# Four small edits in a fused attention and mixture-of-experts kernel: the order of two projections, one layout, one operand's memory, one copy's loop order

## The chip, the cores and the metric

The kernel runs on one core of one Trainium2 chip. The metric is the device time of one execution in microseconds (us). The core has TensorE (PE, matrix products; PEld are its weight loads), VectorE (DVE), ScalarE (ACT), GpSimd (POOL) and SyncE (SP, which issues the DMA transfers here). Each engine works through its own queue in order, and engines wait for each other by semaphores. SBUF is the on-chip memory of 128 partitions, PSUM the memory into which TensorE writes.

## The reference

The input x is (2, 128, 256, 256): two images of 128 channels. Everything is fp32.

```python
x = x + conv(ln_c(x), W_qkv, W_out, rel_height, rel_width)
t = to_tokens(x)                       # (2, 65536, 128)
t = t + ffn(ln_t(t), router_w, router_b, expert_w, expert_b)
x = from_tokens(t)
```

`conv` is windowed attention with 4 heads of 32 channels: queries from windows of 8 x 8 pixels, keys and values from overlapping windows of 12 x 12, relative position logits by height and width computed from the query, softmax, then an output projection. A fixed mask leaves only the pairs of query and key whose rows have the same parity and whose columns have the same parity, so the attention splits into four independent planes, one for each parity of row and column. `ffn` is a mixture of 8 experts (128 x 128 matrices): a softmax router, the two best experts for each token, their weights normalised to one. `ln_c` and `ln_t` subtract the mean over the 128 channels and divide by the standard deviation.

## The kernel before, in words

Channels lie on the 128 partitions. An image is cut into 32 strips of 8 pixel rows; a strip has four planes of 4 x 128 positions (`NQ` = 512). The main loop (line 809) makes one turn per plane, 256 in all, and 7 more at the end. In every turn n four things at different stages of the pipeline go on side by side:

- `scores` and `attend` of plane n: 16 matmuls (L474) put the relative position logits into PSUM with `keys` (a 0/1 matrix that spreads them) as the stationary and `au` as the moving operand; 64 matmuls (L491) add queries times keys; ScalarE takes the exponential (L499, `pT`); 8 matmuls (L512) give the row sums, 64 (L522) the weighted values. DVE then transposes and inverts the sums (L532 `sT`, L534, L537 `rT`) and scales (L542, `o`). The arrays are used in tiles: 4 heads on 32 partitions each, two halves of the windows beside each other.
- `project` of plane n + 1: the bias logits `pu` (L408), the value rows `pv` (`value_rows`, L350), the keys `pk` (L423) and the queries `pq` (L445), each a PSUM tile from the pool `ps_mm`, which has three buffers that are used in turn. Their readers: `uT`, a DVE transpose (L413), of `pu`; `vr`, a ScalarE copy (L358), of `pv`; `kcol`, ScalarE copies (L434, and L441 for the edges), of `pk`; `qs`, a ScalarE copy (L447), of `pq`. The same pool serves `plt` and `plg` (norms) and `po` (output projection), so a turn normally takes seven buffers in the order pu, pv, pk, pq, plt, plg, po.
- `shift` of plane n + 1: two copies (L392) move parts of `uT` into `auT`, and a DVE transpose (L397) makes `au`. The stream transpose turns blocks of 32 x 32.
- `norms`, `route`, `spread` and the expert products for pixel rows of the strips before. `norms` lets TensorE sum x and x squared over the channels (L580, `plt`), transposes the sums into another PSUM tile (L589, `plg`), and `rstd` (L222) makes the reciprocal standard deviation: L232 to L235 form the variance u plus eps, ScalarE takes a logarithm and an exponential (L236, L237), and L238, L239, L596 and L598 do one Newton step. `route` picks the experts (L613 to L645). `spread` (L648) transposes the gates (L651, `gT`) and sends them to DRAM (`gd`), from where SP fetches them broadcast to all partitions (`gb`, `sb`, `rb`). DVE makes six products `xe` of the tokens with a gate (L705), GpSimd two more, and TensorE multiplies them with the eight expert matrices (L714), summing in PSUM (`acc`); L720 adds the sum to x. Each fp32 matmul shows as two passes with a weight load each.

The order within a turn is written out by hand (`tc.manual_schedule`, L808): each engine's queue holds its instructions in the order in which the generator steps in lines 826 to 902 issue them. On TensorE it is: scores, pu, pv, pk, pq, experts 4, 6, 7, 5 of the strip under way, row sums and attention products, plt, experts 0, 1, 2 of the next, po, expert 3. On DVE: router, gT, uT, auT, au, xs, xe, sT to o, plg, `rstd`, the addition of po (L555). On GpSimd: product 5, the normalisation of a row for a coming strip (L276, `ln1`), in one turn of four a copy of halo rows (L250), product 7. A one-element write to the buffer (L686, L688) stands before each transfer of a gate, so that the transfer starts no earlier than that point of the ScalarE or DVE queue. SP's queue takes gd, the value rows to DRAM (L369, `vrows`), rb, sb, the value windows back (L381, `vwin`) and the gates.

`rstd` keeps u and r in SBUF tiles of 128 x 8. `au` has the layout (window m of 32, row a, column s), so that L474's moving operand is 8 pieces of 16 consecutive elements, while the transpose L397 writes with a step of 16 elements. `kcol` holds the keys of a pair of windows as 10 columns of 6 rows; L434 writes row by row, each element 6 behind the one before.

Of the kernel before, what the change touches and what calls it, by code (L numbers as in the profile page):

```python
# [11 lines left out]
F32 = mybir.dt.float32  # L12
AF = mybir.ActivationFunctionType
ALU = mybir.AluOpType
# [3 lines left out]
P = 128  # L18
# [25 lines left out]
KR, KC = 6, 10  # L44
# [7 lines left out]
def kernel(  # L52
# [16 lines left out]
    nc = tc.nc  # L69
    B, C, H, W = x.shape  # L70
    NS = H // R
    PR, PC = R // 2, W // 2
    NP = PC // 8
# [18 lines left out]
    def mm_tile(name):  # L92
        return ps_mm.tile([P, 512], F32, tag="mm", name=name)
# [121 lines left out]
    auT = []  # L215
# [3 lines left out]
        nc.gpsimd.memset(auT[i][:, :, :, KR + 6 : KR + 7], NEG)  # L219


    def rstd(p4, k0, k1, name):  # L222

        u, r = (
            small.tile([P, 2, NT], F32, tag=v, name=f"{v}_{name}")[:, k0:k1] for v in ("u", "r")
        )
        mean, sq = (
            p4[:, :, E + 2 * k0 + j : E + 2 * k1 : 2].rearrange("p t k -> p k t") for j in range(2)  # L230
        )
        nc.vector.tensor_copy(r, mean)  # L232
        nc.vector.tensor_tensor(u, r, mean, ALU.mult)
        nc.vector.scalar_tensor_tensor(u, u, -1.0, sq, ALU.mult, ALU.add)
        nc.vector.scalar_tensor_tensor(u, u, 0.0, epsc[:, k0:k1], ALU.max, ALU.add)  # L235
        nc.scalar.activation(r, u, AF.Ln, scale=4.0)  # L236
        nc.scalar.activation(r, r, AF.Exp, scale=-0.5)  # L237
        nc.vector.scalar_tensor_tensor(u, u, -4.0, r, ALU.mult, ALU.mult)  # L238
        nc.vector.tensor_tensor(u, u, r, ALU.mult)  # L239
        return r, u  # L240
# [145 lines left out]
    def shift(uT, n, state):  # L386

        for j in range(2):
            shifted = uT[:, :, :, NU * j + 3 : NU * j + 9]
            dims = [list(d) for d in shifted.ap]  # L390
            dims[1 + j][0] -= 1
            nc.vector.tensor_copy(  # L392
                auT[n % 2][:, :, :, 6 * j : 6 * j + 6],
                bass.AP(shifted.tensor, shifted.offset, dims),
            )
        au = work.tile([P, 2 * NP, PR, 4], F32, tag="au", name=f"au{n}")
        nc.vector.transpose(au.rearrange("p m a s -> p a s m"), auT[n % 2])  # L397
        state["au"] = au

    def project(n, state):  # L400

        i, pl = divmod(n, 4)
        xp = xn[i % 2][:, pl // 2, pl % 2]
        inner = xp[:, 1 : 1 + PR, 1 : PC + 1]
        kk = kcol[pl]

        pu = mm_tile(f"pu{n}")
        nc.tensor.matmul(pu, lhsT=wrel, rhs=inner, start=True, stop=True)  # L408
        state["sent"] = value_rows(n)
        yield  # L410

        uT = work.tile([P, PR, 4, 32], F32, tag="uT", name=f"uT{n}", bufs=1)
        nc.vector.transpose(uT, pu.rearrange("p (a m s) -> p a s m", a=PR, s=4))  # L413
        state["shift"] = lambda: shift(uT, n, state)
        yield

        rows = list(ln_rows(i))
        for part in (rows[-4:], rows[:-4]):
            if not part:
                continue  # L420
            pk = mm_tile(f"pk{n}_{part[0]}")
            m = len(part)
            nc.tensor.matmul(  # L423
                pk[:, : m * PC],
                lhsT=wk,
                rhs=xp[:, part[0] : part[0] + m, 1 : PC + 1],
                start=True,
                stop=True,
            )
            pk3 = pk[:, : m * PC].rearrange("p (r c) -> p r c", r=m)  # L430
            for k, at, m in runs(i, part):
                new = pk3[:, k - part[0] : k - part[0] + m]
                places = kk[:, :, 0:NK].rearrange("p t (c r) -> p t r c", r=KR)[:, :, at : at + m]
                nc.scalar.copy(places[:, 1 : NP - 1], windows(new[:, :, KC - 3 :], 0, NP - 2))  # L434

                ends = [places[:, 0, :, 1:], new[:, :, 0 : KC - 1]]
                for j, step in enumerate(((NP - 1) * SLOT - KR, PC - KC + 1)):
                    dims = [list(d) for d in ends[j].unsqueeze(1).ap]
                    dims[1] = [step, 2]
                    ends[j] = bass.AP(ends[j].tensor, ends[j].offset, dims)  # L440
                nc.scalar.copy(*ends)  # L441
        yield

        pq = mm_tile(f"pq{n}")
        nc.tensor.matmul(pq, lhsT=wq, rhs=inner, start=True, stop=True)  # L445
        qs = work.tile([P, 2 * NP, PR, 4], F32, tag="qs", name=f"qs{n}")
        nc.scalar.copy(  # L447
            qs.rearrange("p m a s -> p a m s"), pq.rearrange("p (a m s) -> p a m s", a=PR, s=4)
        )
        yield  # L450

        state.update(qs=qs, kk=kk, vv=vwin[n % 2])
        yield

    def windows(rows, n0, count):

        first = rows[:, :, 8 * n0 : 8 * n0 + KC].unsqueeze(1)
        dims = [list(d) for d in first.ap]
        dims[1] = [8, count]
        return bass.AP(first.tensor, first.offset, dims)  # L460

    def scores(n, state):


        qs, kk, au = state["qs"], state["kk"], state["au"]
        turn = place(n // 4, 0) // 2
        att = ps_att.tile([P, 4, 512], F32, tag="att", name=f"att{n}")
        sc = att[:, :, 0:HQ]
        for w in range(2):
            for half in range(2):  # L470
                rows = slice(half * SLOT, (half + 1) * SLOT)
                for h in range(HEADS):
                    hp = slice(h * DH, (h + 1) * DH)
                    nc.tensor.matmul(  # L474
                        sc[rows, h].rearrange("p (t w z) -> p t w z", w=2, z=16)[:, :, w],
                        lhsT=keys[hp, turn, w],
                        rhs=au[hp, half * NP + w : (half + 1) * NP : 2].rearrange(
                            "p t a s -> p t (a s)"
                        ),
                        start=(w == 0),  # L480
                        stop=False,
                    )
        for t in range(HP):
            if t == HP // 2:
                yield
            for half in range(2):
                rows = slice(half * SLOT, (half + 1) * SLOT)
                m0 = 2 * (half * HP + t)
                for h in range(HEADS):
                    hp = slice(h * DH, (h + 1) * DH)  # L490
                    nc.tensor.matmul(  # L491
                        sc[rows, h, 32 * t : 32 * t + 32],
                        lhsT=kk[hp, half * HP + t, :],
                        rhs=qs[hp, m0 : m0 + 2].rearrange("p m a s -> p (m a s)"),
                        start=False,
                        stop=(t == HP - 1),
                    )
        pT = work.tile([P, HEADS, HQ], F32, tag="pT", name=f"pT{n}", bufs=1)
        nc.scalar.activation(pT, att[:, :, 0:HQ], AF.Exp)  # L499
        state.update(att=att, pT=pT)  # L500
        yield
# [61 lines left out]
    def norms(f, c, nm):  # L563

        g = gboth[next(g_turn) % len(gboth)]
        srcs = []
        for j, src in ((0, f and rows_of(*f)), (2, c and ln1_src(*c))):  # L570
            if src is None:
                continue
            sq = work.tile([P, CH], F32, tag=f"sq{j}", name=f"sq{j}{nm}", bufs=1)
            nc.scalar.activation(sq, src, AF.Square)  # L574
            srcs += [(j, src), (j + 1, sq)]
        yield
        plt = mm_tile(f"plt{nm}")
        for j, src in srcs:
            for t in range(NT):
                nc.tensor.matmul(  # L580
                    plt[32 * t : 32 * t + 32, :P],
                    lhsT=rw[:, j],
                    rhs=src[:, t * P : (t + 1) * P],
                    start=(j == srcs[0][0]),
                    stop=(j == srcs[-1][0]),
                )
        yield
        plg = mm_tile(f"plg{nm}")
        nc.vector.transpose(plg[:, :P], plt[:, :P])  # L589
        p4 = plg[:, :P].rearrange("p (t e) -> p t e", e=32)  # L590
        k0, k1 = (0 if f else 1), (2 if c else 1)
        r, u = rstd(p4, k0, k1, nm)
        rs = None
        if f:
            rs = small.tile([P, NT], F32, tag="rs", name=f"rs{nm}")
            nc.vector.scalar_tensor_tensor(rs, u[:, 0], 3.0, r[:, 0], ALU.add, ALU.mult)  # L596
        if c:
            nc.vector.scalar_tensor_tensor(  # L598
                g[:, 1, :, 1], u[:, 1 - k0], 3.0, r[:, 1 - k0], ALU.add, ALU.mult
            )  # L600
        yield g, rs, p4
# [360 lines left out]
```

## Time and profile before

| what | value |
|---|---|
| median of three runs | 4380.1 us (4376.23 to 4390.58) |
| the profiled execution | 4380.58 us |
| its span in the profile | 4378.8 us |
| mean TensorE clock granted | 0.993 of full |
| TensorE busy | 4248.2 us, 97% |
| TensorE weight loads | 2454.2 us, 56% |
| VectorE busy | 3853.9 us, 88% |
| ScalarE busy | 1456.6 us, 33% |
| GpSimd busy | 1091.6 us, 25% |
| DMA | 1022.19 MB, 233 GB/s in the mean |

The span is that of one execution recorded by the hardware profiler; the time of that execution is 1.8 us longer, for what lies around it. A group of instructions is named by line, engine, operation and tiles (out<-in), followed by shapes, count, busy time, mean time of one, and the idle time of the engine ahead of it with what ended that idle time. In the timeline each row has start and length in us, and in square brackets how long the engine was idle before and what released it. Matmuls are pipelined, and their ends are modelled: a row of TensorE includes its way through the array, so starts tell more than ends.

### The profile page before, as it was taken

To read this page: it belongs to the slowest core of one execution; us is meant where nothing else is said; L and a number is where in the kernel's file an instruction comes from. 1 tells how busy PE (TensorE), PEld (TensorE's weight loads), DVE (VectorE), ACT (ScalarE), POOL (GpSimd) and SP (SyncE) were. 2 spreads that over 40 slices of the span, in tenths; PEclk is the share of its full clock that TensorE was granted. 3 is DMA by queue.
4 is the path that set the end of the run, shared out by engine and by line. 5 is a ranking of instruction groups with operands and counts; after the bars stand their busy time and mean duration, and the time that the engine had idled before them with its cause. 6 is when DMAs were issued, how large, how long until landed. Compare 5 with 4: busy or idle time off the path is not lost. (4 is left out here: it accounts for less than half of the span.)

```text
span 4378.8 us, 224652 instructions
## 1 busy us (share of the span) xinstructions
PE 4248.2 (97%) x94273; PEld 2454.2 (56%) x94273; DVE 3853.9 (88%) x11850; ACT 1456.6 (33%) x3774; POOL 1091.6 (25%) x1126
## 2 busy tenths in 40 slices
PE   7899999999999999999999999999999999999987
PEld 5455555555555555555555555555555555555553
DVE  5899889899888989989888889988998888999987
ACT  3333333333333333333333333333333333333321
POOL 1222222222222222222222222222222222222211
PEclk9999999999999999999999999999999999999999
DMA  4677778777777787777777787777777777777766
GB/s 114 210 240 240 244 235 243 241 237 244 233 244 240 244 244 233 243 232 244 238 241 234 240 244 236 243 236 243 238 240 243 236 242 232 244 238 239 243 191 191
DMA packets 824580, 1022.19 MB, mean 233 GB/s; under 512 B 137634, under 2 KB 409634, under 8 KB 823594
## 3 DMA queue, kind: packets, MB, share of 16 engines
q1 hardware_dynamic: 822864, 1007.52, 74.8%
q8 instruction: 769, 12.60, 1.2%
q14 instruction: 217, 1.78, 0.1%
q10 hardware_dynamic: 730, 0.29, 0.0%
HBM read 863.78 MB, written 143.75 MB: 230 GB/s over the span
## 5 line engine op out<-in xcount | busy, mean ns | idle before, releaser
L714 PE MATMUL acc<-xe,ew 128*128 128x512 f32 x4096 | 1916.8, 600 | 21.4 <-DVE gb L688 17.5
L714 PEld LDWEIGHTS acc<-xe,ew 128*128 128x128 f32 x4096 | 757.9, 190 | 941.4 <-issue 872.1
L705 DVE TENSOR_TENSOR xe<-xs,gb 128x512 f32<-128x512 f32 x1536 | 950.5, 686 | 11.8 <-DMA gb<-gd 1.4
L709 POOL COPY last<-xe 128x1 f32<-128x1 f32 x256 | 47.0, 184 | 3088.0 <-DVE gb L688 3081.0
L705 POOL TENSOR_TENSOR xe<-xs,gb 128x512 f32<-128x512 f32 x512 | 650.7, 1272 | 0.7 <-issue 0.5
L276 POOL TENSOR_TENSOR xn<-xt,rb 128x512 f32<-128x512 f32 x249 | 373.7, 1501 | 170.4 <-DMA rb<-gd 164.1
L491 PE MATMUL att<-qs,kcol 32*64 32x32 f32 x32768 | 398.2, 227 | 5.1 <-issue 5.1
L491 PEld LDWEIGHTS att<-qs,kcol 32*64 32x64 f32 x32768 | 395.9, 131 | 6.6 <-issue 6.2
L522 PEld LDWEIGHTS att<-pT,vwin 64*32 64x32 f32 x32768 | 350.2, 105 | 50.4 <-issue 11.8
L522 PE MATMUL att<-pT,vwin 64*32 64x32 f32 x32768 | 350.6, 200 | 8.0 <-issue 6.3
L350 PEld LDWEIGHTS pv<-wt,xn 128*128 128x128 f32 x2048 | 270.1, 192 | 126.5 <-issue 78.7
L434 ACT COPY kcol<-pk 128x560 f32<-128x560 f32 (+2 forms) x344 | 319.0, 927 | 52.8 <-PE pk L423 49.4
L499 ACT ACTIVATE pT<-att 128x1024 f32<-128x1024 f32 x256 | 261.8, 1023 | 208.0 <-PE att L491 207.2
L445 PE MATMUL pq<-xn,wt 128*128 128x512 f32 x512 | 274.7, 617 | 30.0 <-DVE uT L413 26.0
L574 ACT ACTIVATE sq<-xt 128x512 f32<-128x512 f32 x505 | 291.9, 629 | 0.0
L408 PE MATMUL pu<-xn,wrel 128*128 128x512 f32 x512 | 291.7, 651 | 0.0
L397 DVE STREAM_TRANSPOSE au<-auT 128x512 f32<-128x512 f32 x256 | 272.3, 1064 | 9.0
L550 PE MATMUL po<-o,wt 128*128 128x512 f32 x512 | 264.4, 598 | 8.4 <-DVE o L542 5.8
L350 PE MATMUL pv<-wt,xn 128*128 128x128 f32 x2048 | 271.2, 275 | 0.8 <-issue 0.8
L532 DVE STREAM_TRANSPOSE sT<-att 128x512 f32<-128x512 f32 x256 | 183.5, 717 | 98.7 <-PE att L522 84.7
L423 PE MATMUL pk<-xn,wt 128*128 128x512 f32 (+2 forms) x528 | 262.9, 582 | 1.3 <-DVE uT L413 1.3
L474 PEld LDWEIGHTS att<-au,keys 32*64 32x64 f32 x8192 | 117.9, 133 | 227.8 <-PE po L550 183.5
(2696 smaller groups left out, 4895.9 us busy)
## 6 DMA issues: line engine op xcount, KB each, us to landing
gb<-gd SPq DMA_DIRECT2D x2048, 256.0 KB, 5.8
vwin<-vrows SPq DMA_DIRECT2D x512, 240.0 KB, 5.4
xt<-in_x_dram SPq DMA_DIRECT2D x256, 256.0 KB, 6.6
sb<-gd SPq DMA_DIRECT2D x256, 256.0 KB, 4.1
out_dram<-xt SPq DMA_DIRECT2D x256, 256.0 KB, 6.2
rb<-gd SPq DMA_DIRECT2D x249, 256.0 KB, 3.4
vrows<-vr SPq DMA_DIRECT2D x168, 256.0 KB, 3.9
vrows<-vr SPq DMA_DIRECT2D x160, 128.0 KB, 3.5
```

The source lines that it names most:

```text
L276: eng.tensor_tensor(xn[i % 2][:, :, :, k, 1 : PC + 1], ln1_src(i, k).rearrange("p (y j x) -> p y x j", y=2, x=2), rb.rearrange("p (y j x) ...
L350: nc.tensor.matmul(pv[:, j * P : (j + 1) * P], lhsT=xp[:, k, 1 : PC + 1], rhs=wv, start=True, stop=True,)
L397: nc.vector.transpose(au.rearrange("p m a s -> p a s m"), auT[n % 2])
L408: nc.tensor.matmul(pu, lhsT=wrel, rhs=inner, start=True, stop=True)
L434: nc.scalar.copy(places[:, 1 : NP - 1], windows(new[:, :, KC - 3 :], 0, NP - 2))
L445: nc.tensor.matmul(pq, lhsT=wq, rhs=inner, start=True, stop=True)
L491: nc.tensor.matmul(sc[rows, h, 32 * t : 32 * t + 32], lhsT=kk[hp, half * HP + t, :], rhs=qs[hp, m0 : m0 + 2].rearrange("p m a s -> p (m a ...
L522: nc.tensor.matmul(av[hp, half, 32 * t : 32 * t + 32], lhsT=vv[rows, t, hp], rhs=pT[rows, h, 32 * t : 32 * t + 32], start=True, stop=True,)
L550: nc.tensor.matmul(po, lhsT=wo, rhs=state["o"].rearrange("p f z -> p (f z)"), start=True, stop=True)
L574: nc.scalar.activation(sq, src, AF.Square)
L705: eng.tensor_tensor(self.xe[e], self.xs, self.gb.pop(e), ALU.mult)
L714: nc.tensor.matmul(self.acc, lhsT=ew[:, e, :], rhs=self.xe.pop(e), start=(e == 0), stop=not self.xe)
```

## The change

1. In `project`, `value_rows(n)` is called ahead of the bias matmul `pu`: the order of the buffers becomes pv, pu, pk, pq.
2. `au` gets the layout (a, s, m), in which the transpose L397 writes consecutive elements. The moving operand of L474 becomes a strided view: m in steps of 2 elements, (a, s) in steps of 32 elements as the inner index.
3. `rstd` takes a piece of the PSUM tile `plg` behind its first 128 columns, and keeps u there. The product of the mean with itself goes to an SBUF tile m.
4. L434's copy goes through its elements with the row as the innermost index rather than the column.

The number and the sizes of instructions stay the same. Behind the first edit the lines of the changed file move by one to three.

```diff
-    def rstd(p4, k0, k1, name):
-        u, r = (
-            small.tile([P, 2, NT], F32, tag=v, name=f"{v}_{name}")[:, k0:k1] for v in ("u", "r")
+    def rstd(p4, room, k0, k1, name):
+        u = room.rearrange("p (k t) -> p k t", t=NT)[:, k0:k1]
+        r, m = (
+            small.tile([P, 2, NT], F32, tag=v, name=f"{v}_{name}")[:, k0:k1] for v in ("r", "m")
         )
...
         nc.vector.tensor_copy(r, mean)
-        nc.vector.tensor_tensor(u, r, mean, ALU.mult)
-        nc.vector.scalar_tensor_tensor(u, u, -1.0, sq, ALU.mult, ALU.add)
+        nc.vector.tensor_tensor(m, r, mean, ALU.mult)
+        nc.vector.scalar_tensor_tensor(u, m, -1.0, sq, ALU.mult, ALU.add)
...
-        au = work.tile([P, 2 * NP, PR, 4], F32, tag="au", name=f"au{n}")
-        nc.vector.transpose(au.rearrange("p m a s -> p a s m"), auT[n % 2])
+        au = work.tile([P, PR, 4, 2 * NP], F32, tag="au", name=f"au{n}")
+        nc.vector.transpose(au, auT[n % 2])
...
+        state["sent"] = value_rows(n)
         pu = mm_tile(f"pu{n}")
         nc.tensor.matmul(pu, lhsT=wrel, rhs=inner, start=True, stop=True)
-        state["sent"] = value_rows(n)
...
-                nc.scalar.copy(places[:, 1 : NP - 1], windows(new[:, :, KC - 3 :], 0, NP - 2))
+                nc.scalar.copy(
+                    places[:, 1 : NP - 1].rearrange("p t r c -> p t c r"),
+                    windows(new[:, :, KC - 3 :], 0, NP - 2).rearrange("p t r c -> p t c r"),
+                )
...
-                        rhs=au[hp, half * NP + w : (half + 1) * NP : 2].rearrange(
-                            "p t a s -> p t (a s)"
-                        ),
+                        rhs=au[hp].rearrange("p a s m -> p m (a s)")[
+                            :, half * NP + w : (half + 1) * NP : 2
+                        ],
...
-        r, u = rstd(p4, k0, k1, nm)
+        r, u = rstd(p4, plg[:, P : P + 2 * NT], k0, k1, nm)
```

## The prediction

> **What bounds the kernel now.** I read the busy shares first, then the groups of instructions, then the waits, then the timeline of two turns. A turn is one pass of the loop over the 256 planes.
>
> Page and groups (busy us, mean ns of one, idle before it):
> ```profile
> PE 4248.2 (97%) x94273; PEld 2454.2 (56%) x94273; DVE 3853.9 (88%) x11850; ACT 1456.6 (33%) x3774; POOL 1091.6 (25%) x1126
> ...
> L434 ACT COPY kcol<-pk 128x560 f32<-128x560 f32 (+2 forms) x344 | 319.0, 927 | 52.8 <-PE pk L423 49.4
> L397 DVE STREAM_TRANSPOSE au<-auT 128x512 f32<-128x512 f32 x256 | 272.3, 1064 | 9.0
> L537 DVE STREAM_TRANSPOSE rT<-rc 128x512 f32<-128x512 f32 x256 | 182.1, 711 | 8.9
> L474 PE MATMUL att<-au,keys 32*64 32x128 f32 x8192 | 180.6, 284 | 31.2 <-issue 31.2
> ```
> TensorE is nearly always busy, VectorE (DVE) comes next, ScalarE and GpSimd have room. The one slow form on DVE is L397, 1064 ns against 711 for a transpose of the same size.
>
> Waits (us, times, longest):
> ```profile
> PEld pq L445 <- DVE uT L413: 176.7, 235, 2.0
> DVE sT L532 <- PE att L522: 84.7, 150, 3.7
> ```
> Each of the two engines waits for the other once in a turn: TensorE's pq for DVE's transpose uT (it frees pu's buffer), DVE's sT for the attention products.
>
> Timeline of a short turn, start and length in us:
> ```profile
> 1980.62 0.66 PE L512 MATMUL att<-pT,ones 64*32 64x256 f32 x16
> ...
> 1985.90 0.17 DVE L235 SCALAR_TENSOR_TENSOR u__117_37497<-u__117_37497,epsc 128x8 f32<-128x8 f32 x1
> ...
> 1991.54 0.67 DVE L413 STREAM_TRANSPOSE uT<-pu 128x512 f32<-128x512 f32 x1
> 1991.64 1.02 PE L423 MATMUL pk<-xn,wt 128*128 128x512 f32 x2
> ...
> 1992.50 1.02 PE L445 MATMUL pq<-xn,wt 128*128 128x512 f32 x2
> ...
> 1996.89 0.66 PE L512 MATMUL att<-pT,ones 64*32 64x256 f32 x16
> ```
> From L512 to L512 it takes 16.27 us. pq starts 0.86 us after pk, which is pk's own streaming time: nothing is lost.
>
> Timeline of a longer turn:
> ```profile
> 2014.07 0.66 PE L512 MATMUL att<-pT,ones 64*32 64x256 f32 x16
> ...
> 2018.77 1.27 POOL L705 TENSOR_TENSOR xe<-xs,gb 128x512 f32<-128x512 f32 x1
> ...
> 2019.36 0.70 DVE L235 SCALAR_TENSOR_TENSOR u__119_38135<-u__119_38135,epsc 128x8 f32<-128x8 f32 x1
> ...
> 2025.52 0.67 DVE L413 STREAM_TRANSPOSE uT<-pu 128x512 f32<-128x512 f32 x1
> ...
> 2026.24 0.30 PEld L445 LDWEIGHTS pq<-xn,wt 128*128 128x128 f32 x2 [0.96 <-DVE uT L413]
> ```
> Here L235, on eight numbers, takes 0.70 us and ends at 2020.06, within 0.02 us of GpSimd's product (2018.77 + 1.27). Everything behind it on DVE is late, uT too, and pq starts late. The next L512 is at 2030.73: a turn of 16.66 us.
>
> About a quarter of all turns last 16.27 us. I take that for what TensorE needs by itself. The mean is (4099.31 - 368.16) / 224 turns = 16.66 us. So some 0.39 us a turn is waiting.
>
> [...]
> - [...] all 144 executions of L235 and all 28 of L238 that took over 0.2 us end within 0.06 us of the end of a GpSimd instruction; L234, which reads one operand from PSUM, never exceeds 0.165 us.
> - [...] (1064 - 711) / 512 = 0.69 ns more per element in L397.
> - [...] Here an fp32 pass over 512 columns takes 0.43 us[...].
>
> **The change part by part.** The profiled execution took 4380.58 us, its span 4378.8 us with 1.8 us around it; the median of the runs is 4380.1 us. The sums stand against 4380.6.
>
> *Value rows ahead of bias rows.* Same instructions, other order: pv, pu, pk, pq share three buffers, so pq now follows pv's reader, ScalarE's copy vr, instead of uT. vr waits for pv and for pT ahead of it on ScalarE. In the short turn pT ended at 1990.91; vr takes 0.58 and would be done near 1991.55, before pk has streamed at 1992.50: no wait. If vr were later, the eight expert passes, the row sums and all of the attention products would stand behind pq, so this is the cover to watch. pu now waits for plg's last reader, L621, where pv did; in a short turn it ends 1.8 us before pu's new start. The first weight load after the scores lies open in either order. Behind pq the plt matmuls now need uT, about 6 us later than uT ends. pu itself ends 0.89 us later (the time of pv), near 1991.85, so uT starts about 0.3 us later than in a short turn. That costs DVE, not TensorE, and the shorter L397 gives it back. The vrows transfers keep their place in SP's queue (behind gd, which waits for gT, after pv in both orders); nothing on GpSimd's queue moves.
>
> *The norms' variance in PSUM.* L235, L238, L239 and the two users of u lose their second SBUF input. L235 sums to 107.3 us over 260 and L238 to 59.2; unblocked they would take 260 x 0.166 = 43.2 and 260 x 0.168 = 43.7. That frees 80 us of DVE, 0.31 a turn. ScalarE's Ln reads PSUM instead of SBUF: within 0.05 us either way, by L234 against an unblocked L235; I take 0. What comes late next: the first instruction with two SBUF inputs is then L614, 7.36 us into a turn; GpSimd ends by 6.3 even in turns with the halo copy. None of the 256 executions of L614 is stretched now.
>
> These two edits remove the same loss: either makes pq punctual, so they don't add. Together they should bring turns to 16.27 us. Of 224 x 0.39 = 87 us, some 6 us are the extra rows of the second image's first strip, which stay; some 5 us may come from turns outside that stretch. A little waiting will remain, since DVE in a short turn is only about 0.1 us ahead at sT. **I take 84 us.**
>
> *Plain writes of the last turn.* L397 falls from 1064 to about 711 ns, 90 us of DVE over the run, beside TensorE's pq and expert products: off the path once pq doesn't wait. But the 32 passes of L474 in a turn now read their moving operand in steps of 32 elements, 128 bytes. Eight tiles work side by side, so the array streams 2 x 2 x 128 = 512 columns, 0.43 us, all on TensorE's path. Unknown cost X. Below nothing is excluded: the contiguous read is already at the stream's rate. Lower bound 0. Upper bound: ScalarE's price for stepped elements in L434, (670 - 183) / 280 = 1.74 ns (its form of two rows) against (580 - 183) / 512 = 0.78 of the plain copy vr, 183 ns being ScalarE's copy of one element (L114): 0.96 x 512 = 0.49, say 0.50 us. Between: DVE's price, 0.69 x 512 = 0.35. I take 0: [...] the ones matmuls L512 show four column groups fed from the same rows at once at full rate (16 passes of 0.21 us within 0.46 us), and the penalties that I can measure are on other engines. It is my weakest step.
>
> *Keys column by column.* L434 writes runs of four instead of single elements and reads PSUM in steps of 512 bytes: between 0.6 us and today's 1.2 us for 560 elements; I take 0.65. ScalarE's squares end 2.8 us before plt needs them, so both ends cost nothing; without that cover a slower copy would reach plt only when over 2.8 us longer.
>
> Sum: 4380.6 - 84 + 0 = **4297 us**.
>
> **Rivals.**
> - *The stepped read costs like DVE's (X = 0.35).* 256 x 0.35 = 90 eats the gain: 4387, no change. For it: [...] L397. Against: another engine, a write.
> - *The stepped read runs at half rate or at ScalarE's price* (X = 0.43 to 0.50): the keys phase doubles, 110 to 128 us, 4407 to 4425, slower. It decides from X = 84 / 256 = 0.33 on. For it: L434's elements cost more than twice a plain element's. Against: [...] four column groups coexist.
> - [...] X about 1.3 (four times 0.43): 4297 + 333 = 4630.
> - *DVE stays the pace*: uT waits longer for pu than reckoned, and half of the gain is kept: about 4340. Against: DVE loses 0.31 + 0.35 a turn.
>
> **How the numbers follow.** X near 0: 0.57, with its own range 4280 to 4325. DVE stays: 0.06. X near 0.35: 0.12. Half rate or worse: 0.21. X about 1.3: 0.04. Faster by over 0.3% (13 us, about what a measurement of this kernel can tell from no change) is 0.57 + 0.06 = 0.63; within it 0.12; slower 0.25. The range runs from 4280, where also the last waits go, to 4412, half of the half-rate case: it leaves out about 0.04 + 0.10 above and 0.03 below.
>
> **What would show it.** Right: L512 to L512 at 16.3 us nearly always; no wait of pq for uT; L235 and L238 at 0.16 us; L397 near 0.71; from the start of L474 to the first L491 0.5 us as now. Wrong: that distance at 0.9 us or more, a new wait of DVE's uT for pu over 0.5 us, or pq waiting for vr.

## The result, and the profile after

| | before | after |
|---|---|---|
| median of four runs each, us | 4379.5 (4376.23 to 4390.58) | 4398.62 (4396.73 to 4404.28) |
| profiled execution, us | 4380.58 | 4399.02 |
| span, us | 4378.8 | 4397.2 |
| mean TensorE clock granted | 0.993 | 0.992 |

After to before is 1.0041, with a 95% interval of 1.0021 to 1.0061: the changed kernel is slower, by some 19 us or 0.4%.

The page of after, its line of busy shares and its groups (busy us, mean ns of one, idle before it):

```profile
PE 4314.1 (98%) x94273; PEld 2553.2 (58%) x94273; DVE 3731.8 (85%) x11850; ACT 1320.4 (30%) x3774; POOL 1088.0 (25%) x1126
...
L412 DVE STREAM_TRANSPOSE uT<-pu 128x512 f32<-128x512 f32 x256 | 183.6, 717 | 219.2 <-PE pu L408 219.2
...
L476 PE MATMUL att<-au,keys 32*64 32x128 f32 x8192 | 285.6, 396 | 31.2 <-issue 31.2
...
L433 ACT COPY kcol<-pk 128x560 f32<-128x560 f32 (+2 forms) x344 | 183.0, 532 | 273.4 <-PE pk L422 270.6
```

VectorE and ScalarE gave up what was asked of them: DVE is busy 122 us less (3853.9 to 3731.8), ScalarE 136 us less. TensorE is busy 66 us more with the same 94273 matmuls. The group that grew is L476 (L474 before), the products that spread the bias logits: a matmul lasts 396 ns instead of 284. The time that they keep TensorE busy rose by 105 us (180.6 to 285.6).

The groups again, the other two of DVE's big transposes:

```profile
L396 DVE STREAM_TRANSPOSE au<-auT 128x512 f32<-128x512 f32 x256 | 182.1, 711 | 9.0
L539 DVE STREAM_TRANSPOSE rT<-rc 128x512 f32<-128x512 f32 x256 | 182.1, 711 | 8.8
```

The transpose into `au` now costs exactly what rT costs.

The waits of after (us, times, longest):

```profile
DVE uT L412 <- PE pu L408: 219.2, 255, 14.3
DVE sT L534 <- PE att L524: 67.9, 248, 1.9
PE att L493 <- issue: 1.6, 4, 0.6
```

The wait of TensorE's pq for uT, 176.7 us before, has no row any more. Instead DVE waits for TensorE twice in nearly every turn: 255 times for pu and 248 times for the attention products. TensorE alone now sets the pace.

The variance: busy time and count of L234 (L235 before) between 300 and 4300 us, core's clock and DMA share behind them:

```profile
300.00:4300.00 4000.00, 41.41 (x238) 1.00 0.77 237
```

41.41 / 238 = 0.174 us each, where before 239 of them took 98.13 us in the same stretch, 0.411 us each. None waits for GpSimd any more: the longest of all in after takes 0.175 us.

One turn of after in the timeline (start, length, and in brackets the idle time before and its releaser):

```profile
1856.81 0.66 PE L514 MATMUL att<-pT,ones 64*32 64x256 f32 x16
...
1860.88 1.27 POOL L707 TENSOR_TENSOR xe<-xs,gb 128x512 f32<-128x512 f32 x1
...
1862.10 0.17 DVE L234 SCALAR_TENSOR_TENSOR plg<-plg,epsc 128x8 f32<-128x8 f32 x1
...
1864.03 1.12 PE L476 MATMUL att<-au,keys 32*64 32x128 f32 x32
...
1864.93 1.54 PE L493 MATMUL att<-qs,kcol 32*64 32x32 f32 x128
...
1868.26 1.02 PE L422 MATMUL pk<-xn,wt 128*128 128x512 f32 x2
...
1868.46 0.72 DVE L412 STREAM_TRANSPOSE uT<-pu 128x512 f32<-128x512 f32 x1 [0.67 <-PE pu L408]
...
1869.11 1.02 PE L447 MATMUL pq<-xn,wt 128*128 128x512 f32 x2
...
1873.50 0.66 PE L514 MATMUL att<-pT,ones 64*32 64x256 f32 x16
```

L234 lasts 0.17 us although GpSimd's product ended only 0.05 us after it began. pq starts 0.85 us after pk: punctual. But from the first L476 to the first L493 it takes 0.90 us, and from L514 to L514 16.69. That is not an unusually long turn: 208 of the 256 turns last 16.6 to 16.7 us.

Mean distances between the starts of a turn's phases, from the starts of the matmuls in turns 20 to 243, in us. The last two columns are two experiments of the next section, to which the table will be needed again.

| from the first ... to the first ... | before | after | e1 | e12 |
|---|---|---|---|---|
| bias products (L476) to scores (L493): the keys phase | 0.487 | 0.896 | 0.487 | 0.487 |
| scores to the next projection | 1.495 | 1.480 | 1.564 | 1.457 |
| pk to pq | 1.049 | 0.857 | 0.860 | 0.857 |
| pq to row sums (experts between) | 4.469 | 4.394 | 4.428 | 4.391 |
| attention products to plt | 1.337 | 1.275 | 1.296 | 1.268 |

After against before: 0.409 - 0.015 - 0.192 - 0.075 - 0.062 = +0.065 us a turn, or 16.6 us over 256 turns, of the 18.4 us between the two profiled executions. The pq wait is gone, as forecast, and the stepped read has eaten more than all of it. Yet two rows were not expected to move: the attention products and the expert products of before also lost something in each turn, and the scores of e1, which has no pq wait and no stepped read, lose more than those of before. The experiments had to say what that is.

### The profile page after: what moved, and what is told of

The parts are those of the page before. It is cut to its first block, busy times and chain, and to the rows that moved or that the text cites. A ratio compares the mean times of both kernels' runs of the same rounds, so it can differ in the third digit from the quotient of the medians.

```text
span 4397.2 us, 224393 instructions
## 1 busy us (share of the span) xinstructions
PE 4314.1 (98%) x94273; PEld 2553.2 (58%) x94273; DVE 3731.8 (85%) x11850; ACT 1320.4 (30%) x3774; POOL 1088.0 (25%) x1126
## 3 DMA queue, kind: packets, MB, share of 16 engines
q8 instruction: 769, 12.60, 1.2%
## 5 line engine op out<-in xcount | busy, mean ns | idle before, releaser
L707 DVE TENSOR_TENSOR xe<-xs,gb 128x512 f32<-128x512 f32 x1536 | 951.0, 687 | 12.5 <-DMA gb<-gd 2.1
L493 PEld LDWEIGHTS att<-qs,kcol 32*64 32x64 f32 x32768 | 422.7, 133 | 11.2 <-issue 2.0
L493 PE MATMUL att<-qs,kcol 32*64 32x32 f32 x32768 | 398.8, 225 | 1.8 <-issue 1.6
L412 DVE STREAM_TRANSPOSE uT<-pu 128x512 f32<-128x512 f32 x256 | 183.6, 717 | 219.2 <-PE pu L408 219.2
L476 PE MATMUL att<-au,keys 32*64 32x128 f32 x8192 | 285.6, 396 | 31.2 <-issue 31.2
L349 PE MATMUL pv<-wt,xn 128*128 128x128 f32 x2048 | 301.4, 291 | 0.3 <-issue 0.3
L476 PEld LDWEIGHTS att<-au,keys 32*64 32x64 f32 x8192 | 160.2, 140 | 236.3 <-PE po L552 183.5
L408 PE MATMUL pu<-xn,wrel 128*128 128x512 f32 x512 | 265.3, 600 | 0.2 <-issue 0.2
L433 ACT COPY kcol<-pk 128x560 f32<-128x560 f32 (+2 forms) x344 | 183.0, 532 | 273.4 <-PE pk L422 270.6
L447 PE MATMUL pq<-xn,wt 128*128 128x512 f32 x512 | 261.6, 592 | 0.2 <-issue 0.2
L349 PEld LDWEIGHTS pv<-wt,xn 128*128 128x128 f32 x2048 | 252.1, 194 | 11.1 <-issue 0.7
```

The costliest lines, as they stand in the source:

```text
L349: nc.tensor.matmul(pv[:, j * P : (j + 1) * P], lhsT=xp[:, k, 1 : PC + 1], rhs=wv, start=True, stop=True,)
L476: nc.tensor.matmul(sc[rows, h].rearrange("p (t w z) -> p t w z", w=2, z=16)[:, :, w], lhsT=keys[hp, turn, w], rhs=au[hp].rearrange("p a s ...
L493: nc.tensor.matmul(sc[rows, h, 32 * t : 32 * t + 32], lhsT=kk[hp, half * HP + t, :], rhs=qs[hp, m0 : m0 + 2].rearrange("p m a s -> p (m a ...
L707: eng.tensor_tensor(self.xe[e], self.xs, self.gb.pop(e), ALU.mult)
```

## The experiments

The theory before the first run (A): the stepped read of edit 2 costs 0.41 us a turn, and the rest brings 84 us. The rival (B): the read costs little, and the plain write, the moved order or a new wait takes the time. Later a third came up (C): TensorE's own instruction stream arrives late. All ratios are to the kernel before on the same chip, with 95% intervals; its medians on the chips used lay between 4384 and 4398 us.

### Edit 2 undone

```diff
-        au = work.tile([P, PR, 4, 2 * NP], F32, ...)
-        nc.vector.transpose(au, auT[n % 2])
+        au = work.tile([P, 2 * NP, PR, 4], F32, ...)
+        nc.vector.transpose(au.rearrange("p m a s -> p a s m"), auT[n % 2])
...
-        rhs=au[hp].rearrange("p a s m -> p m (a s)")[:, half * NP + w : (half + 1) * NP : 2]
+        rhs=au[hp, half * NP + w : (half + 1) * NP : 2].rearrange("p t a s -> p t (a s)")
```

> The changed kernel with the second edit undone: au is again written in steps by the transpose and read in pieces of 16 consecutive elements; the other three edits stay. Theory A (the stepped read of the moving operand runs at half rate, 0.42 us in every turn, and all else went as forecast): turns of 16.27 us, 4398.6 - 256 x 0.42 = 4291 us; keys phase (start of the bias products to start of the scores) 0.49 us instead of 0.90. Theory B (the new order paces the turn: DVE's uT waits for pu, 219 us in all): turns stay near 16.69 us, 4398 us, since the DVE work even grows by 0.35 us a turn.

Measured: 4329.9 us, 0.9872 (0.9857 to 0.9886). B falls. But A is off too: edits 1, 3 and 4 together gain 54 us, not 84 or more, and from after to e1 the span shrinks by 66 us (4397.2 to 4330.8), though the keys phase shortened by 0.409 us, 105 us over 256 turns. In 149 of 256 turns e1 reaches 16.27 us; the rest is longer, and the table above says where: 0.107 us a turn in the scores above e12's 1.457. A long turn of e1 in its timeline:

```profile
1697.90 0.66 PE L514 MATMUL att<-pT,ones 64*32 64x256 f32 x16
...
1705.13 0.69 PE L476 MATMUL att<-au,keys 32*64 32x128 f32 x32
...
1705.61 0.37 PE L493 MATMUL att<-qs,kcol 32*64 32x32 f32 x17
...
1706.38 1.34 PE L493 MATMUL att<-qs,kcol 32*64 32x32 f32 x111 [0.40 <-issue]
1706.38 1.23 PEld L493 LDWEIGHTS att<-qs,kcol 32*64 32x64 f32 x110 [0.50 <-issue]
```

TensorE stops in the middle of a run of 128 equal matmuls, behind the 17th, and it waits for nothing that the profile shows: the releaser reads "issue". This is the view that gave theory C.

### The read alone, and the write alone

The stepped read on the old layout, and the plain write with a contiguous read:

```diff
 # e2_read_alone, against before
-        rhs=au[hp, half * NP + w : (half + 1) * NP : 2].rearrange("p t a s -> p t (a s)")
+        rhs=au[hp].rearrange("p m a s -> p (m a s)").rearrange("p (z m) -> p m z", m=2 * NP)[
+            :, half * NP + w : (half + 1) * NP : 2]
 # e3_write_alone, against after
-        rhs=au[hp].rearrange("p a s m -> p m (a s)")[:, half * NP + w : (half + 1) * NP : 2]
+        rhs=au[hp].rearrange("p a s m -> p (a s m)").rearrange("p (m z) -> p m z", z=PR * 4)[
+            :, half * NP + w : (half + 1) * NP : 2]
```

> The kernel before with one thing changed: the bias products read au in steps of 32 elements, while the transpose still writes as before (the position logits are thus permuted, only their time is of interest). Theory A: keys phase 0.90 us instead of 0.49 in every turn. The short turns of 16.27 us become 16.69; turns that DVE paces (above 16.69) absorb the 0.42, since the bias products lie on TensorE between two waits, so that the mean rises by about 0.15 us: 4419 us, at most 4380 + 107 = 4487. Theory B: 4380 us, unchanged.

Measured: 4442.77 us, 1.0131 (1.0116 to 1.0146). The keys phase is 0.896 us, as in after: the read makes all of it. The loss is 58 us, more than the 39 forecast, but not 105. Of the difference of 47 us, 26 are pq's wait, which shrinks meanwhile (pk to pq 0.946 us instead of 1.049), presumably because DVE gets time to catch up. Most of the rest lies at the borders of the instruction blocks, of which a later part tells: 78 ns a turn are lost there in e2, and 146 in before.

> The changed kernel, with the plain writes of the transpose kept but a read of 16 consecutive elements (the position logits are permuted, only their time is of interest). Theory A: 4291 us like the kernel with the old layout: the 0.35 us that the transpose saves per turn lie on DVE beside TensorE and are worth nothing, less than 0.2%. If DVE shared the pace, it would be up to 90 us faster than the old layout. Theory B: 4398 us.

Measured: 4328.72 us, 0.9870 (0.9855 to 0.9884), as e1 (0.9872). The plain write takes 90 us off DVE and is worth nothing to the time.

### Where the read becomes dear

Three more patterns for the same 512 elements. e4 keeps the values of after, but lets the window be the inner index: the read goes in steps of 8 bytes, and PSUM is written in steps of 128 bytes. e5 and e6 read other elements of `au`, in steps of 8 and of 16 bytes, and write PSUM as after does.

```diff
 # e4_window_inner
-        sc[rows, h].rearrange("p (t w z) -> p t w z", w=2, z=16)[:, :, w],
+        sc[rows, h].rearrange("p (t w z) -> p z t w", w=2, z=16)[:, :, :, w],
-        rhs=au[hp].rearrange("p a s m -> p m (a s)")[:, half * NP + w : (half + 1) * NP : 2]
+        rhs=au[hp].rearrange("p a s m -> p (a s) m")[:, :, half * NP + w : (half + 1) * NP : 2]
 # e5_step2, k = 2; e6_step4, k = 4
+        rhs=au[hp].rearrange("p a s m -> p (a s m)")[:, 0 : 128 * k].rearrange(
+            "p (t z k) -> p t z k", t=HP, k=k)[:, :, :, w]        # e6: 2 * half + w
```

> The changed kernel, with the order of the 128 columns of a bias product turned: the window is the inner index, so that the moving operand is read in steps of 2 elements (8 bytes) and the product is written to PSUM in steps of 32 elements (128 bytes). Same values. Theory A with the penalty on the reading side alone: keys phase 0.49 us, 4291 us. If a stepped write to PSUM costs as much as the stepped read did: 0.90 us, 4398 us; if more, above. Theory B: 4398 us.

> The changed kernel, with the moving operand of the bias products read in steps of 2 elements, 8 bytes (other elements of au than the right ones, so the position logits are wrong; the product is written as before). [...] keys phase 0.49 us, time as with the old layout, about 4330 us. If any step costs: 0.90 us, 4398 us.

> The same with steps of 4 elements, 16 bytes[...]. [...] keys phase 0.90 us and about 4398 us, like steps of 128 bytes. If only long steps cost: 0.49 us and about 4330 us.

Measured: e4 4338.14 us, 0.9892 (0.9876 to 0.9909); e5 4332.52, 0.9884 (0.9858 to 0.9910; two runs); e6 4407.09, 1.0056 (1.0036 to 1.0077; three runs). The rows of L476 in e4, e5 and e6, one kernel a fence:

```profile
L476 PE MATMUL att<-au,keys 32*64 32x128 f32 x8192 | 190.0, 292 | 31.3 <-issue 31.3
```

```profile
L476 PE MATMUL att<-au,keys 32*64 32x128 f32 x8192 | 185.0, 286 | 31.2 <-issue 31.2
```

```profile
L476 PE MATMUL att<-au,keys 32*64 32x128 f32 x8192 | 294.9, 406 | 30.7 <-issue 30.7
```

292 and 286 ns with steps of 8 bytes, 406 with steps of 16. The keys phase says the same: 0.527, 0.511 and 0.928 us against 0.487 contiguous and 0.896 with steps of 128 bytes. So the price rises somewhere between steps of 8 and of 16 bytes, and a step of 128 costs no more than one of 16 (396 ns against 406). At 16 bytes the phase takes about double (0.928 / 0.487 = 1.9). No run here tells why: whether the length of the step decides or how close together the elements lie was not shown (pairs of neighbours with gaps between the pairs were not tried). Stepping the writes to PSUM cost little: with steps of 128 bytes there, e4's phase is 0.016 us longer than e5's (0.527 against 0.511).

### Twice the columns, contiguous

The old layout of e1, and every bias product streams 256 contiguous columns, twice the work:

```diff
-        sc[rows, h].rearrange("p (t w z) -> p t w z", w=2, z=16)[:, :, w],
+        sc[rows, h],
-        rhs=au[hp, half * NP + w : (half + 1) * NP : 2].rearrange("p t a s -> p t (a s)")
+        rhs=au[hp, half * NP : (half + 1) * NP].rearrange("p m a s -> p (m a s)")
```

> The old-layout kernel in which each bias product streams all 256 columns of its half instead of every second group of 16, read contiguously: twice the columns with the same number of instructions (the position logits are then wrong). If a stepped column takes the time of two and nothing else is special about it: keys phase 0.90 us, the stalls in the scores fall from 0.108 to about 0.01 us a turn because the late blocks have 0.41 us more, and the time is that of the changed kernel, 1.0041 of before within 0.3%. If the small stalls of the changed kernel came from its stepped reads or its other DVE work: the stalls stay at 0.17 us a turn, 4330 + 105 = 4435 us.

Measured: 4412.71 us, 1.0034 (1.0021 to 1.0047). Its row of L476:

```profile
L476 PE MATMUL att<-au,keys 32*64 32x256 f32 x8192 | 292.8, 393 | 32.6 <-issue 32.1
```

393 ns for 256 contiguous columns, 396 for 128 stepped ones: a stepped element takes the time of two columns. And the kernel is near after (1.0034 against 1.0041), with an equally long keys phase (0.914 us) that has nothing to do with strides: lengthening that phase by 0.41 us is enough to give the time of after.

### Where the rest went: the borders of the instruction blocks

Among the DMA queues of after is one for instructions (packets, MB, share of 16 engines' time):

```profile
q8 instruction: 769, 12.60, 1.2%
```

12.60 MB / 769 are 16,384 bytes a packet, and 769 packets are three in each of 256 turns and one more. A turn has 368 matmuls with a weight load each, 736 instructions, and L825 (L823 before; not part of the change) pads every turn from n = 6 to 255 to three blocks of 256:

```python
BLOCK, FIRST_LIMIT = 256, 99
...
nc.tensor.addr_align(BLOCK, offset=BLOCK - FIRST_LIMIT)
```

The count fits if these packets are TensorE's instructions, 256 in each. Then a turn should cross a border into a new block behind 99, 355 and 611 instructions, that is behind its matmuls 49, 177 and 305. In the timeline of e1 above the stop is behind 32 + 17 = 49. For 216 turns of each kernel whose records are complete, I took from every step between the starts of neighbouring matmuls the tenth percentile of that same step, as its undisturbed length; the mean of what is left I count as lost time. It stands out at these places and, in before, at pq (ns a turn); all other steps have 15 ns or less, but for five of 26 to 30 ns in e7:

| behind matmul | before | after | e1 | e7 | e8 | e12 | e14 |
|---|---|---|---|---|---|---|---|
| 49 (in the scores) | 38 | 12 | 106 | 93 | 29 | 0 | 4 |
| 177 (in the experts) | 27 | 8 | 37 | 6 | 50 | 0 | 0 |
| 305 (in the attention products) | 81 | 12 | 38 | 26 | 159 | 1 | 1 |
| 172 and 173 (pq) | 233 | 1 | 1 | 0 | 4 | 0 | 0 |

The table agrees with the length of the turns: in these 216, before, e1 and e8 take 0.370, 0.186 and 0.220 us longer than e12, and their entries sum to 0.379, 0.182 and 0.242. A step of the scores that lies 16 further on (behind 65) loses 0 to 2 ns in each of these kernels. And the matmuls behind the steps that lost over 100 ns start within a narrow range of time behind the landing of a block: in e1 at 49, 46 steps, 1.23 to 1.57 us (median 1.41) behind it; in before at 305, 55 steps, 1.20 to 1.58 (median 1.42). Of the other steps at these two places, none ended sooner than 1.24 us behind the last landing. I call a block late when TensorE has to wait for this time behind its landing.

*The borders moved.* e1, with the first border 31 instructions later:

```diff
-BLOCK, FIRST_LIMIT = 256, 99
+BLOCK, FIRST_LIMIT = 256, 130
```

> The kernel with the old layout (4330 us), with the alignment of each turn's TensorE instructions moved by 31: the three borders between 16 KB blocks of instructions fall 130, 386 and 642 instructions after the start of the bias products instead of 99, 355 and 611. Theory C (what is left of waiting in the old-layout kernel is TensorE waiting for the next block of its own instructions): the second border now lies in the row sums, 1.6 us ahead of the third, against some 2 to 4 us from a block's border to the landing of the next one; so TensorE stalls in the attention products nearly every turn by about 1 us: 4500 to 4650 us. Theory D (the waiting comes from data that arrive late): the numbers of instructions ahead of a border don't matter, 4330 us.

Measured: 4331.66 us, 0.9876 (0.9855 to 0.9898). The forecast of C was missed widely, and the time is the one that D gave: I had taken it that the fetch starts when the border before is reached. But by D the places should have stayed, and they went with the borders: behind matmul 49 e11 loses 0 ns, behind matmul 65 (130 / 2) 102; behind 305 1, behind 321 36. Only the middle border, 193, costs nothing there.

*Less data beside the blocks.* e1, and e14 after, without the way of the value rows to DRAM and back in the loop:

```diff
-            if n + 1 < n_planes:
-                send_values(n + 1, states[n + 1]["sent"])
...
-            if n + 1 < n_planes:
-                take_values(n + 1)
```

> The old-layout kernel without the transfers of value rows to DRAM and back inside the loop (vrows and vwin, about 0.74 of 3.8 MB a turn; the attention uses stale values, so its output is wrong). Theory C, with the blocks late because they queue behind data: they land sooner, the stalls in the scores fall from 0.108 us a turn to under 0.05, the mean turn from 16.47 to about 16.33: 4330 - 35 = 4295 us. If the blocks are late for another reason: 4330 us.

> The changed kernel without the transfers of value rows to DRAM and back (stale values in the attention, so its output is wrong). Against the old-layout kernel without them (0.9779 of before, 4287 us, no stalls left) only the layout differs: turns of 16.69 instead of 16.27 us, 105 us more, 4392 us, hardly below the changed kernel itself (its stalls were 0.03 us a turn). If the layout costs less where there are no late blocks: below 4370 us.

Measured: e12 4287.09 us, 0.9779 (0.9759 to 0.9800); e14 4392.91, 0.9989 (0.9980 to 0.9998). TensorE's instructions are the same. The traffic falls from 1022.2 to 829.9 MB, by a fifth, and the number of packets by more than a third (e1 in the first fence, e12 in the second):

```profile
DMA packets 824578, 1022.17 MB, mean 236 GB/s; under 512 B 137634, under 2 KB 409634, under 8 KB 823594
```

```profile
DMA packets 522871, 829.92 MB, mean 194 GB/s; under 512 B 124512, under 2 KB 129312, under 8 KB 521896
```

The waits for nothing inside the scores, in e1 (first fence) and e12 (second), us, times, longest:

```profile
PE att L493 <- issue: 15.9, 30, 1.4
...
PEld att L493 <- issue: 19.6, 34, 1.5
```

```profile
PE att L493 <- issue: 1.8, 2, 1.0
```

What changes for the blocks is above all when they start to move: the third block of a turn starts 13.4 us behind the turn's first bias product in e1 (median; 15.7 at the 95th percentile), and 12.5 (13.3) in e12, while its transfer takes 1.19 and 0.96 us. In e12 234 of 256 turns last 16.27 us, and no border costs anything: this is the turn that the forecast gave for after. The turns of e12 and e14 differ by 16.69 - 16.27 = 0.42 us, the stepped read bare: about 107 us. The two profiled spans differ by 4391.1 - 4284.5 = 106.6 (they come from two chips, on which the median of before differed by 13 us; as ratios to before they differ by 0.0210, or 92 us). With the value trip the same read costs only 4397.2 - 4330.8 = 66.4 us (after against e1; as ratios 0.0169, or 74 us).

### The edits alone

```diff
 # e7_order_alone, against before
+        state["sent"] = value_rows(n)
         pu = mm_tile(f"pu{n}")
         nc.tensor.matmul(pu, lhsT=wrel, rhs=inner, start=True, stop=True)
-        state["sent"] = value_rows(n)
```

e8 is before with edit 3 (the variance in `plg`), e9 with edits 1 and 3, e10 with edit 4 (the key copy), each as in the diff of the change.

> The kernel before with the first edit alone (value rows ahead of bias rows). Forecast theory: pq no longer waits for uT, and that by itself takes most of the gain of edits 1 and 3: 4330 to 4350 us against 4384 before on the same chip. DVE still loses 0.31 us a turn to GpSimd; with its work of 16.3 us a turn it can just keep up. If DVE's stalls still pace the turn: 4384 us.

> The kernel before with the third edit alone (the variance in PSUM). Forecast theory: L235 and L238 are never stretched, uT is punctual, pq waits only after a turn in which TensorE lost time elsewhere: 4330 to 4350 us. If the waiting of pq has another cause than the stalls of DVE: 4384 us.

> The kernel before with the first and the third edit. They remove the same loss, so both together: 4330 us, not 54 us less than either alone; and equal within 0.2% to the old-layout kernel, which has the fourth edit too.

> The kernel before with the fourth edit alone (keys copied column by column). The copy of 560 elements falls from 1.18 to about 0.65 us on ScalarE, which nobody waits for: 4384 us, within 0.3%.

| | us | ratio | 95% |
|---|---|---|---|
| e7, edit 1 | 4328.58 | 0.9857 | 0.9836 to 0.9877 |
| e8, edit 3 | 4350.01 | 0.9898 | 0.9880 to 0.9916 |
| e9, edits 1 and 3 | 4336.62 | 0.9869 | 0.9854 to 0.9884 |
| e10, edit 4 | 4392.66 | 1.0001 | 0.9990 to 1.0012 |

Edit 1 alone gives as much as edits 1 and 3 together, or as 1, 3 and 4 in e1 (the intervals overlap): edit 3 brings nothing on top, edit 4 nothing at all. Each of edits 1 and 3 takes the 233 ns of pq away; in e8 the borders take back 92 of them (29 + 50 + 159 = 238 ns against 38 + 27 + 81 = 146 before). Apart from e12, which leaves out the way of the value rows, the version to keep is before with edit 1: 1.4% faster than before, and so ahead of after as well.

## Why the prediction was wrong

**The step that failed: "I take 0" for the stepped read, in "Plain writes of the last turn".** X is 0.896 - 0.487 = 0.41 us a turn. That lies between its bounds, 0 and 0.50, next to the rival "half rate" (0.43). The argument for 0 didn't hold: the four column groups on the same rows at once (L512's 16 passes of 0.21 us within 0.46) didn't keep a stepped element from costing a whole column more (e13: 393 ns for 256 contiguous columns, 396 for 128 stepped ones in after). DVE's price for stepped elements, (1064 - 711) / 512 = 0.69 ns, would have given 0.35, the near rival.

**The 84 us of edits 1 and 3, a mis-sized term.** The mechanism was right: L234 and L237 are never stretched (41.41 and 41.52 us over 238 each), pq never waits for uT, either edit alone does it, and e12's turns are 16.27 us as read from the short turns of before. The size was wrong where "I take that for what TensorE needs by itself" turned into "some 0.39 us a turn is waiting", and all of this was booked on pq. Of before's waiting, 233 ns a turn were pq's and 146 the borders'. In e1 the first went to 1 and the second rose to 106 + 37 + 38 = 181: a net gain of 197 ns, 50 us over 256 turns, with 54 measured. "What comes late next" named GpSimd and L614; it was TensorE's own instructions.

**Why the sum nevertheless fits with X put in.** 4380.6 - 84 + 256 x 0.41 = 4401.6, and 4399.0 was measured. That is luck: the sum's 84 us were pq's wait alone, while in after pq gave up 232 ns a turn and the borders 114, together 89 us. The borders cost 12 + 8 + 12 = 32 ns only in after. e13, with its long keys phase by other means, loses little too (36 + 4 + 27 = 67 ns), and so does e6 (9 + 7 + 19 = 35). So the long keys phase spares about 149 of the 181 ns that e1 loses: 105 - 38 = 67 us net, against 66 measured. For the first border the reason is likely that matmul 49 comes 0.41 us later, when most late blocks are there; why less is lost at the other two as well isn't shown.

**L396** fell to 711 ns as forecast, and e3 shows that it was worth nothing in time. The price of stepped output was right for DVE, and beside the path. L397 in before, which writes in steps of 64 bytes, took 1064 ns, 0.69 ns more an element than the plain write.

**uT's wait for pu** was forecast at 0.3 us; it is (219.2 - 14.3) / 254 = 0.81 in after and 0.67 in the turn shown. DVE waits there for a TensorE that is 0.41 us longer; in e1 it is (136.9 - 15.0) / 251 = 0.49. It costs nothing in either, since pq no longer waits for uT.

**pq behind vr**: no wait, as forecast. **Edit 4**: the copy of 560 elements takes 0.64 us instead of 1.19 (means of 168 of them), and the time doesn't move (e10), as forecast.

**What stays open.** What makes the fetch of a block begin isn't known: e11's missed forecast shows that it isn't the border before. The three blocks of a turn start to move at the same points in e11 as in e1 (medians 3.7, 7.5 and 13.4 us behind its first bias product, each within 0.1), though in e11 TensorE reaches the middle border 2.5 us later. That the blocks come late because of the transfers beside them follows from e12 and e14 (1 and 5 ns a turn lost at the borders, against 181 in e1 and 32 in after); which of them holds the blocks up wasn't separated, nor whether it is their bytes, the number of their packets or their place in the queues, nor why edit 3 alone drives the borders of the attention products up to 159 ns. A kernel that keeps all transfers and lacks the late blocks was not tried.

## What to carry to other kernels

A layout that spares one engine its stepped writes hands the steps to the reader: count them on the engine that sets the pace; here, fp32 elements 16 or 128 bytes behind the one before cost TensorE about the time of two columns (406 and 396 ns for 128 elements; 393 for 256 contiguous ones, 284 for 128). Before all waiting is booked on one releaser, split it by place, position by position within a turn; stops in the middle of equal instructions without a releaser belong to something else, and ending the wait for that releaser need not end them. A gain measured beside such stops isn't additive, in either direction: here a slowdown ahead of them hid them (32 ns a turn in after, 67 in e13), and a speedup laid them bare (181 in e1 and 238 in e8, 146 in before).

## What the runs showed of the hardware

- An fp32 moving operand whose elements lie 8 bytes apart streamed at nearly the contiguous rate (a keys phase of 0.511 us in e5 against 0.487 in e1), at 16 and at 128 bytes at about half of it (0.928 in e6 and 0.896 in after).
- Stepping the PSUM side of these fp32 matmuls by 128 bytes added 0.016 us to a keys phase of 0.511 (e4 against e5).
- The instruction queue q8 moved 769 packets of 16,384 bytes, 12.60 MB (after). Where TensorE's instruction behind a border of 256 was late, it started 1.2 to 1.7 us after a packet's landing (with one exception in some 900 late starts). A turn of 736 instructions lost 32 to 238 ns to late blocks in the kernels with all transfers. In e12, without the value trip, it lost 1 ns; in e1 181, some 46 us over 256 turns.
- ScalarE's copy of 560 elements from PSUM took 0.64 us with runs of four written (and read in steps of 512 bytes; L433 in after), and 1.19 with single elements written 24 bytes apart (L434 in before).
